# A four-layer graph network on one core: propagation slabs cut into 6-block pieces, and three small moves in TensorE's order

## The chip, the cores and the metric

The kernel runs on one core of one Trainium2 chip. The metric is the device time of one execution in microseconds; the time given for the kernel is the median of three runs. One execution was also taken with the hardware profiler, and every view quoted below comes from that one.

## The reference, cut to what matters

The input is x (3327 nodes of 256 features) and a dense adjacency matrix adj of 3327 x 3327, in float32. Each of four layers has the form x = x + layer(relu(layernorm(x)), adj):

```python
# layer 0:  adj @ (h @ W.T + b)
# layer 1:  relu(keep(tanh(adj * adj)) @ (tanh(h @ Wp + bp) @ Wg) + bg)   # keep: 700 largest of each row
# layer 2:  relu(A_norm @ (h @ W.T)),  A_norm = d^-1/2 (adj + I) d^-1/2
# layer 3:
R = S + jnp.eye(N); R = R / R.sum(-1, keepdims=True)      # S is adj
for n in range(2):
    A  = _top_p_attention(Xa, W1, W2, W3)   # softmax of q @ k.T, smallest set of 0.9, renormalized
    Xf = R @ Xf
    Xa = A @ Xa
    Z  = Z + Xf @ U1[n].T + Xa @ U2[n].T
# then layernorm(X + Z)
```

The change touches layer 3, where every step has a product with R ("propagation") and a product with the attention matrix A, and the order of a few steps in layers 1 and 2.

## The kernel before, in words

The 3327 nodes are padded to T = 26 row blocks of P = 128; H = 13 is half of that. The products of 26 x 26 blocks are done in halves of 13 blocks by a seven-product scheme: sums of quarter matrices are formed once and multiplied in products numbered 1 to 7, and the results are added up.

TensorE (PE) executes in an order that the program writes out by hand; the other engines' instructions are ordered by a scheduler at build time, from the program's priorities. All loads of R's blocks are issued on SyncE's (SP's) queue, in order: an issue that waits for a buffer holds up those behind it.

**Layers 0 to 2.** `products()` goes through H = 13 pairs of row blocks; a pair p is one `Product` in three cuts of the inner dimension (`CUTS`). Work of the pair before (turning its result with transposes, L418; projecting it) is hung into the current product's sequence as "hooks": a dictionary from step number to a function, called when PE's program reaches that step. For p = 1, part of whose product is already done during p = 0 (`early`), the hooks are carried into product p = 2, at the steps 10 and 34, and a counting hook at 22.

**Layer 3, first step.** Row block m of the attention is processed as follows. PE makes the logits (L1062), ScalarE (ACT) their exponentials (L1087), VectorE (DVE) finds the threshold and leaves the kept exponentials e_a (L1164). PE turns e_a block by block (L204), ACT copies the turned blocks to eT_a (L207), and PE multiplies them with the node features (L215). `rows.begin(m)` starts this with the first turned blocks, `rows.finish(m)` does the rest. After that the result's `turn`, `node` and `values` make the row's new keys and its share of Z.

Between the rows stand the phases of the propagation. `FirstPropagation(d)` for d = 0 to 5 is a "double", which handles two row blocks of each half at once; d = 6 is the "single". A double has four phases, groups of the seven products:

```python
OF_DOUBLE = (1, 2), (5, 4), (6, 3), (7,)
OF_LAST_DOUBLE = (1, 2), (5, 4), (6,), (3, 7)
OF_SINGLE = (1, 2, 5, 4), (6, 3, 7)
```

A phase of two products has 26 units, one of a single product 13; a unit of a double reads 128 KB of a slab and one of the single 64 KB. `propagate_first(n, at)` does phase n % 4 of double n // 4, with hooks `at` given on a scale of 26. The phases n = 0 to 3 run first, with little between them; n = 4 to 21 alternate with rows; n = 22 to 25 come with the last rows. In the alternating ones the hooks are, in this order, `a.turn`, the next row's preparation, `a.node`, `a.values` and `rows.begin(m + 1)`. After a phase, `keep()` adds its result up on DVE.

A slab of R comes from `adj_t` or, for products of sums of quarters, from `s_dram`, where layer 2 stored these sums. Where the slab has blocks of the diagonal, GpSimd (POOL) adds the identity to them (L1258). `load_slab` issues the DMA (L1253). The pool `slabs` has three buffers of 13 blocks, 832 KB each. A double cuts a product at `(0, 6, 12, 13)`: two slabs of 768 KB, and a last one for k = 12, shared by the phase's products, which takes a whole buffer too. Its units are sorted so that k = 12 comes last. The single and the pairs of step 2 use one slab of 832 KB for a product.

**Layer 3, second step.** The same attention per row; the propagation is done by `propagated_steps` (two row blocks) and by 12 `PropagatedPair` objects, each in two phases of 52 and 39 units that lie between rows.

The functions that the change touches:

Of the kernel before, what the change touches and what calls it, by code (L numbers as in the profile page):

```python
# [11 lines left out]
F32 = mybir.dt.float32  # L12
# [5 lines left out]
ALU = mybir.AluOpType  # L18
# [4 lines left out]
D = 256  # L23
# [7 lines left out]
H = T // 2  # L31
CUTS = ((0, 5), (5, 9), (9, 13))
TOPK = 700
TOP_P = 0.9
# [13 lines left out]
def kernel(  # L48
# [27 lines left out]
    keys = ctx.enter_context(tc.tile_pool(name="keys", bufs=1))  # L76
    slabs = ctx.enter_context(tc.tile_pool(name="slabs", bufs=3))
    ps_tr = ctx.enter_context(tc.tile_pool(name="ps_tr", bufs=2, space=PSUM))
# [78 lines left out]
    def slab_tile(name):  # L157
        return slabs.tile([P, H, P], F32, tag="slab", name=name)

# [134 lines left out]
    def layers_0_to_2(again):  # L294
# [343 lines left out]
        def products(layer, width, rhs, feed, finish, before, pair_after, following=None, counted=None, begin=None):  # L638
# [5 lines left out]
            for p in range(H):  # L644
# [4 lines left out]
                else:  # L649
# [8 lines left out]
                    if early and p == 1:  # L658
                        hooks, carried = {}, {10: todo[0], 34: todo[1]}
                    elif early and p == 2:  # L660
                        hooks.update(carried)
                    if counted and early and p == 1:
                        carried[22] = functools.partial(counted, p)
                    elif counted:
                        hooks[62] = functools.partial(counted, p)
# [331 lines left out]
    def layer_3_in(again, tag, big, ep, w3, sm3, h3, kT0, ksum0, left):  # L997
# [181 lines left out]
        def failed(step, st):  # L1179
# [27 lines left out]
            return levels  # L1207

        def propagated_steps(acc, step, m, xf):

            slab = {}
            order = [k for k in range(T) if k % H < H - 1] + [H - 1, T - 1]
            for n, k in enumerate(order):
                g, j = k // H, k % H
                if g not in slab:
                    s = slab[g] = slab_tile(f"slab3{tag}_{step}_{m}_{g}")
                    nc.sync.dma_start(s, adj_t[m, :, g * H : (g + 1) * H, :])
                    if m // H == g:
                        nc.gpsimd.tensor_tensor(s[:, m - g * H, :], s[:, m - g * H, :], ident, ALU.add)
                nc.tensor.matmul(acc[:, :D], slab[g][:, j, :], xf[:, k, :], start=(n == 0), stop=(n == T - 1))  # L1220
                yield n
# [3 lines left out]
        OF_DOUBLE = (1, 2), (5, 4), (6, 3), (7,)  # L1225
        OF_LAST_DOUBLE = (1, 2), (5, 4), (6,), (3, 7)
        OF_SINGLE = (1, 2, 5, 4), (6, 3, 7)
# [38 lines left out]

        class FirstPropagation:

            def __init__(self, d):
                self.d, self.p = d, 2 * d
                self.q = min(self.p + 2, H)
                self.many = self.q - self.p
                self.width = self.many * P
                self.phases = OF_SINGLE if self.many == 1 else OF_LAST_DOUBLE if d == DOUBLES - 1 else OF_DOUBLE
                self.cuts = (0, H) if self.many == 1 else (0, 6, 12, H)
                self.slabs, self.ys = {}, []
                self.name = f"0{tag}_{d}"

            def load(self, phase, n, c=0):
                a, b = self.cuts[c : c + 2]
                x = slab_tile(f"slab3{tag}_{self.name}_{n}_{c}")
                ns = self.phases[phase] if c == 2 else (n,)
                with tc.issue_after(slabs_behind[-1].ins) if slabs_behind else nullcontext():
                    for i, n in enumerate(ns):
                        part = x[:, i * self.many * (b - a) : (i + 1) * self.many * (b - a), :]
                        self.slabs[n, c] = part.rearrange("p (t k) m -> p t k m", t=self.many)
                        load_slab(self.slabs[n, c], n, self.p, self.q, a, b)

            def units(self, phase):
                units = [(n, k) for n in self.phases[phase] for k in range(H)]
                if self.many > 1:
                    units.sort(key=lambda u: u[1] == H - 1)
                return units

            def steps(self, phase):

                units = self.units(phase)
                place = {n: i for i, n in enumerate((2, 1, 4, 5) if self.many == 1 and not phase else  # L1300
                                                    {1: (2, 1), 5: (4, 5)}.get(units[0][0], self.phases[phase]))}
                self.acc = new_acc(f"f{self.name}_{phase}")
                self.at = {n: slice(c * self.width, (c + 1) * self.width) for n, c in place.items()}
                for at, (n, k) in enumerate(units):
                    c = sum(k >= b for b in self.cuts[1:-1])
                    if (n, c) not in self.slabs:
                        self.load(phase, n, c)
                    nc.tensor.matmul(  # L1308
                        self.acc[:, self.at[n]], right_half(h3, ts, n, k), self.slabs[n, c][:, :, k - self.cuts[c], :],
                        start=not at, stop=at == len(units) - 1, skip_group_check=True,  # L1310
                    )
                    yield at

            def keep(self, phase):
# [5 lines left out]
                with tc.high_priority():  # L1320
                    for k in range(0, len(ns), 2) if ns[0] == 1 or ns[0] == 5 else ():
                        y = w3.tile([P, 2, 2 * P], F32, tag="xf", name=f"y_{self.name}_{phase}_{k}", bufs=3)[:, :, :width]
                        self.ys.append(y)
                        nc.scalar.copy(
                            y, self.acc[:, k * width : (k + 2) * width].rearrange("p (n f) -> p n f", n=2)
                        )
                    for n in ns if ns[0] in (3, 6, 7) else ():
                        (y0, y1), b = self.ys, self.acc[:, self.at[n]].rearrange("p (n f) -> p n f", n=1)
                        if n == 6:
                            nc.vector.tensor_tensor(y0[:, 0:1, :], y0[:, 0:1, :], y0[:, 1:2, :], ALU.add)  # L1330
                            nc.vector.tensor_tensor(y0[:, 1:2, :], y0[:, 1:2, :], b, ALU.add)
                            nc.vector.tensor_tensor(y1, y1, both(y0[:, 1:2, :]), ALU.add)
                        elif n == 3:
                            nc.vector.tensor_tensor(y0[:, 1:2, :], y1[:, 1:2, :], b, ALU.add)
                        else:
                            nc.vector.tensor_tensor(y1, y1, both(b), ALU.add)
                if phase == len(self.phases) - 1:
                    for i, y in enumerate(self.ys):
                        for t in range(self.many):
                            props.append(PropagationOfFirstStep(self.p + t + i * H, y[:, :, t * P : (t + 1) * P]))  # L1340

        class PropagatedPair:


            def __init__(self, step, p, h, ts):
                self.step, self.p, self.h, self.ts = step, p, h, ts
                self.accs, self.slabs, self.name = {}, {}, f"{step}{tag}_{p}"
                self.last = p == H - 1

            def load(self, n):  # L1350
                x = self.slabs[n] = slab_tile(f"slab3{tag}_{self.step}_{self.p}_{n}")
                self.loaded = load_slab(
                    x.rearrange("p (t k) m -> p t k m", t=1), n, self.p, self.p + 1, 0, H
                )

            def steps(self, phase):

                units = [(n, k) for n in PHASES[phase] for k in range(H)]
                place = {**PLACE3, 3: (2, 0)} if self.last else PLACE3
                last = {place[n][0]: (n, k) for n, k in units}  # L1360
                for at, (n, k) in enumerate(units):
                    bank, c = place[n]
                    start = bank not in self.accs
                    if start:
                        self.accs[bank] = new_acc(f"f{self.name}_{bank}")
                    if n not in self.slabs:
                        self.load(n)
                    nc.tensor.matmul(
                        self.accs[bank][:, c * P : (c + 1) * P], self.slabs[n][:, k, :],
                        right_half(self.h, self.ts, n, k),  # L1370
# [316 lines left out]
        with tc.manual_schedule(engines=PE_ALONE):  # L1687
# [38 lines left out]
            firsts, fs = {}, []  # L1726

            def propagate_first(n, at):

# [68 lines left out]
            for m in range(T):  # L1798
# [11 lines left out]
                if interleaved:  # L1810
                    left_over = {}
                    steps, n = prepare(0, m + AHEAD, kT0), next(propagated)
                    at = (4, 14, 18, 22, 24) if n % 4 == 3 else (3, 10, 15, 18, 20)
                    what = a.turn, lambda: next(steps), a.node, a.values, lambda: rows.begin(m + 1)
# [229 lines left out]
```

## Time and profile before

| what | value |
|---|---|
| time, median of three runs | 2498.07 us (2497.99 to 2499.03) |
| profiled execution | 2498.93 us |
| its span | 2497.0 us |
| mean granted clock of PE | 0.998 |
| PE busy | 2471.1 us, 99% of the span |
| DVE busy | 2094.2 us, 84% |
| ACT busy | 1075.8 us, 43% |
| POOL busy | 287.6 us, 12% |
| DMA queue 1 | 367.53 MB, 45.8% of 16 engines |

The span is the profiler's time from the first to the last instruction; the execution's own time is 1.9 us longer. A busy share is an average over the whole kernel. Layers 0 to 2 take the span up to about 935 us, the first step of layer 3 up to about 1770, the second step the rest. "Idle before" in PE's timeline is time in which PE had no instruction in work, with what it waited for; these are the places to look at, since PE is busy for nearly all of the span.

### The profile page before, as it was taken

To read this page: it belongs to the slowest core of one execution; us is meant where nothing else is said; L and a number is where in the kernel's file an instruction comes from. 1 tells how busy PE (TensorE), PEld (TensorE's weight loads), DVE (VectorE), ACT (ScalarE), POOL (GpSimd) and SP (SyncE) were. 2 spreads that over 40 slices of the span, in tenths; PEclk is the share of its full clock that TensorE was granted. 3 is DMA by queue.
4 is the path that set the end of the run, shared out by engine and by line. 5 is a ranking of instruction groups with operands and counts; after the bars stand their busy time and mean duration, and the time that the engine had idled before them with its cause. 6 is when DMAs were issued, how large, how long until landed. Compare 5 with 4: busy or idle time off the path is not lost. (4 is left out here: it accounts for less than half of the span.)

```text
span 2497.0 us, 45220 instructions
## 1 busy us (share of the span) xinstructions
PE 2471.1 (99%) x16719; PEld 2187.2 (88%) x16719; DVE 2094.2 (84%) x5506; ACT 1075.8 (43%) x2109; POOL 287.6 (12%) x488
## 2 busy tenths in 40 slices
PE   9999999999999999999999999999999999999998
PEld 8999999999999997777777777777788888888887
DVE  7876788889888778888788797885899999999995
ACT  3101034443111115566566565663555655555551
POOL 2000010000000000000000000000022222332222
PEclk9999999999999999999999999999999999999999
DMA  6777765555688756323232323323533343344333
GB/s 202 228 231 239 222 199 179 181 175 181 227 304 294 258 192 214 103 80 104 84 96 83 120 67 115 103 64 121 179 115 114 125 142 114 117 140 143 125 118 115
DMA packets 196737, 387.90 MB, mean 155 GB/s; under 512 B 19997, under 2 KB 79898, under 8 KB 196506
## 3 DMA queue, kind: packets, MB, share of 16 engines
q1 hardware_dynamic: 175242, 367.53, 45.8%
q10 hardware_dynamic: 21264, 17.39, 2.1%
q8 instruction: 133, 2.18, 0.4%
q14 instruction: 98, 0.80, 0.1%
HBM read 315.24 MB, written 67.89 MB: 153 GB/s over the span
## 5 line engine op out<-in xcount | busy, mean ns | idle before, releaser
L207 ACT COPY eT_a<-pt_a 128x512 f32<-128x512 f32 (+1 forms) x364 | 196.3, 554 | 375.9 <-PE pt_a L204 373.5
L215 PE MATMUL a<-h3a,eT_a 128*128 128x256 f32 x1352 | 322.0, 381 | 3.2 <-ACT eT_a L207 3.2
L215 PE MATMUL a<-vs,eT_a 128*128 128x256 f32 x1352 | 320.2, 381 | 0.2 <-ACT eT_a L207 0.2
L215 PEld LDWEIGHTS a<-h3a,eT_a 128*128 128x128 f32 x1352 | 246.0, 189 | 48.3 <-issue 10.0
L1149 DVE MAX8 cand_a<-w 128x8 f32<-128x128 f32 x1352 | 284.6, 278 | 3.9
L215 PEld LDWEIGHTS a<-vs,eT_a 128*128 128x128 f32 x1352 | 244.9, 190 | 30.2 <-ACT eT_a L207 0.7
L602 PE MATMUL acc_a<-tsa,s_a 128*128 128x128 f32 (+1 forms) x2028 | 270.1, 275 | 0.0
L602 PE MATMUL acc_a<-tsa,a_a 128*128 128x128 f32 x2028 | 252.9, 276 | 0.0
L602 PEld LDWEIGHTS acc_a<-tsa,s_a 128*128 128x128 f32 x2028 | 249.0, 192 | 0.7
L602 PE MATMUL acc_a<-rhs,a_a 128*128 128x128 f32 (+1 forms) x2028 | 248.6, 276 | 0.0
L602 PEld LDWEIGHTS acc_a<-tsa,a_a 128*128 128x128 f32 x2028 | 241.1, 193 | 0.5
L602 PEld LDWEIGHTS acc_a<-rhs,a_a 128*128 128x128 f32 x2028 | 236.7, 192 | 0.6
L1145 DVE SCALAR_TENSOR_TENSOR w<-e_a,t_a 128x896 f32<-128x896 f32 x208 | 224.8, 1081 | 3.6
L1087 ACT ACTIVATE e_a<-pl_a 128x1024 f32<-128x1024 f32 x260 | 184.5, 728 | 43.5 <-PE pl_a L1062 43.4
L204 PE MATMUL pt_a<-ident,e_a 128*128 128x128 f32 x1352 | 198.4, 272 | 1.4 <-DVE e_a L1164 1.4
L1136 DVE SCALAR_TENSOR_TENSOR w<-e_a,t_a 128x3328 uint8<-128x3328 f32 x52 | 192.1, 3695 | 4.8 <-DVE t_a L1133 0.5
L1164 DVE SCALAR_TENSOR_TENSOR e_a<-e_a,all_least 128x3328 f32<-128x3328 f32 x52 | 192.1, 3695 | 1.8
L204 PEld LDWEIGHTS pt_a<-ident,e_a 128*128 128x128 f32 x1352 | 166.4, 141 | 31.1 <-issue 1.8
L422 ACT ACTIVATE xT_a<-pt_a 128x512 f32<-128x512 f32 x52 | 30.8, 593 | 334.5 <-PE pt_a L418 272.0
L754 ACT ACTIVATE a_a<-a_a 128x640 f32<-128x640 f32 (+1 forms) x156 | 101.6, 666 | 163.8 <-DVE a_a L752 149.8
L1308 PE MATMUL f0a<-slab3a_0a,tsa 128*128 128x256 f32 (+1 forms) x728 | 163.2, 368 | 3.8 <-POOL slab3a_0a L1258 2.5
L1120 ACT ACTIVATE junk_a<-e_a,t_a 128x3328 uint8<-128x3328 f32 x52 | 159.8, 3073 | 1.0 <-POOL parts_a L1082 0.6
(265 smaller groups left out, 4036.7 us busy)
## 6 DMA issues: line engine op xcount, KB each, us to landing
a_a<-in_adj_t_dram SPq DMA_DIRECT2D x312, 256.0 KB, 4.1
a_a<-in_adj_t_dram SPq DMA_DIRECT2D x156, 320.0 KB, 4.0
slab3a<-s_dram SPq DMA_DIRECT2D x48, 832.0 KB, 4.4
slab3a_0a<-s_dram SPq DMA_DIRECT2D x48, 768.0 KB, 4.7
slab3a<-in_adj_t_dram SPq DMA_DIRECT2D x40, 832.0 KB, 4.6
slab3a_0a<-in_adj_t_dram SPq DMA_DIRECT2D x36, 768.0 KB, 4.5
s_dram<-s_a SPq DMA_DIRECT2D x78, 256.0 KB, 5.0
s_dram<-s_a SPq DMA_DIRECT2D x39, 320.0 KB, 4.8
```

The costliest lines, as they stand in the source:

```text
L204: nc.tensor.transpose(pt[:, j, :], e[:, k * P : (k + 1) * P], ident)
L207: last_turned.append(nc.scalar.copy(eT[:, : len(blocks), :], pt[:, : len(blocks), :]))
L215: nc.tensor.matmul(acc[:, :width], ready[g][:, j, :], rhs[:, k, :], start=(k == 0), stop=(k == T - 1))
L602: nc.tensor.matmul(self.acc[:, g, at : at + wide], quads[n][:, k - CUTS[c][0], :], t, start=(k == 0 and n in (1, 4)), stop=(k == H - 1 and ...
L754: nc.scalar.activation(a, a, AF.Tanh)
L1087: last_exp.append(nc.scalar.activation(dst, src, AF.Exp, accum_out=parts[:, c : c + 1]))
L1120: nc.scalar.activation(junk_a, e, AF.Relu, scale=-1.0, bias=t, accum_out=short)
L1136: nc.vector.scalar_tensor_tensor(junk, e, t, e, ALU.is_lt, ALU.mult, accum_out=got)
L1145: nc.vector.scalar_tensor_tensor(w[:, : (b - a) * P], eg, t, eg, ALU.is_lt, ALU.mult, accum_out=below[:, g : g + 1])
L1149: nc.vector.max(cand[:, 8 * k : 8 * k + 8], w[:, (k - a) * P : (k - a + 1) * P])
L1164: nc.vector.scalar_tensor_tensor(e, e, least, e, ALU.is_ge, ALU.mult, accum_out=st["kept"][:, m : m + 1])
L1308: nc.tensor.matmul(self.acc[:, self.at[n]], right_half(h3, ts, n, k), self.slabs[n, c][:, :, k - self.cuts[c], :], start=not at, stop=at = ...
```

## The change

Five things are done:

1. The slabs' pool gets six buffers of 6 blocks (`PIECE = 6`) in place of three of 13. A phase's units are cut into pieces of 6 blocks, which is 3 units of a double or 6 of the single or a pair, whichever product they belong to. A piece that runs over the end of a product takes two DMAs. The units of a phase run in the order of the products; the sorting of k = 12 to the end is left only in the first phase of d = 0. A new class `Pieces` does this for `FirstPropagation` and `PropagatedPair`.
2. In the last double the phase `(6,)` becomes the second, before `(5, 4)`, so n = 21 has 13 units and n = 22 has 26. `keep()` splits its additions accordingly.
3. The hooks carried into product p = 2 in layers 1 and 2 move from steps 10, 34 and 22 to 18, 42 and 30.
4. In phases of one product (n % 4 = 3 before, and now n = 21 as well) `rows.begin(m + 1)` is called at 22 and `a.values` at 24, in place of the other way round.
5. Ahead of the single, four pieces are loaded in place of two slabs.

```diff
-    slabs = ctx.enter_context(tc.tile_pool(name="slabs", bufs=3))
+    slabs = ctx.enter_context(tc.tile_pool(name="slabs", bufs=6))
...
-        return slabs.tile([P, H, P], F32, tag="slab", name=name)
+        return slabs.tile([P, PIECE, P], F32, tag="slab", name=name)
...
-                        hooks, carried = {}, {10: todo[0], 34: todo[1]}
+                        hooks, carried = {}, {18: todo[0], 42: todo[1]}
...
-                        carried[22] = functools.partial(counted, p)
+                        carried[30] = functools.partial(counted, p)
...
-        OF_LAST_DOUBLE = (1, 2), (5, 4), (6,), (3, 7)
+        OF_LAST_DOUBLE = (1, 2), (6,), (5, 4), (3, 7)
...
+        class Pieces:
+            def load(self, phase, s):
+                units = self.units(phase)
+                per = PIECE // self.many
+                x, at = slab_tile(f"slab3{tag}_{self.name}_{phase}_{s}"), 0
+                for n, group in itertools.groupby(units[s * per : (s + 1) * per], lambda u: u[0]):
+                    for a, b in runs(k for _, k in group):
+                        size = self.many * (b - a)
+                        part = x[:, at : at + size, :].rearrange("p (t k) m -> p t k m", t=self.many)
+                        self.loaded = load_slab(part, n, self.p, self.p + self.many, a, b)
+                        for k in range(a, b):
+                            self.slabs[phase, n, k] = part[:, :, k - a, :]
+                        at += size
+
+            def block(self, phase, at):
+                n, k = self.units(phase)[at]
+                if (phase, n, k) not in self.slabs:
+                    self.load(phase, at // (PIECE // self.many))
+                return self.slabs[phase, n, k]
...
             def units(self, phase):
                 units = [(n, k) for n in self.phases[phase] for k in range(H)]
-                if self.many > 1:
+                if not self.d and not phase:
                     units.sort(key=lambda u: u[1] == H - 1)
                 return units
...
                     nc.tensor.matmul(
-                        self.acc[:, self.at[n]], right_half(h3, ts, n, k), self.slabs[n, c][:, :, k - self.cuts[c], :],
+                        self.acc[:, self.at[n]], right_half(h3, ts, n, k), self.block(phase, at),
...
+                        if n == 6 and y1 is not None:
                             nc.vector.tensor_tensor(y1, y1, both(y0[:, 1:2, :]), ALU.add)
...
+                    if phase and self.phases[phase - 1] == (6,):
+                        y0, y1 = self.ys
+                        nc.vector.tensor_tensor(y1, y1, both(y0[:, 1:2, :]), ALU.add)
...
-                    at = (4, 14, 18, 22, 24) if n % 4 == 3 else (3, 10, 15, 18, 20)
+                    at = (4, 14, 18, 24, 22) if len(products_of(n)) == 1 else (3, 10, 15, 18, 20)
...
-            for n in OF_SINGLE[0][:2]:
-                firsts[DOUBLES].load(0, n)
+            for s in range(4):
+                firsts[DOUBLES].load(0, s)
```

`propagated_steps` cuts its 26 units in the same way.

More of the change, by code (lines that the diff above doesn't have):

```diff
@@ L32 @@
 CUTS = ((0, 5), (5, 9), (9, 13))
+PIECE = 6
 TOPK = 700
@@ L1207, in failed, with runs @@
             return levels
+        def runs(ks):
+            out = []
+            for k in ks:
+                if out and out[-1][1] == k:
+                    out[-1][1] += 1
+                else:
+                    out.append([k, k + 1])
+            return out
         def propagated_steps(acc, step, m, xf):
-            slab = {}
             order = [k for k in range(T) if k % H < H - 1] + [H - 1, T - 1]
             for n, k in enumerate(order):
[L1214 to L1220, printed above, removed]
+                j = n % PIECE
+                if not j:
+                    piece = order[n : n + PIECE]
+                    s, at = slab_tile(f"slab3{tag}_{step}_{m}_{n}"), 0
+                    for a, b in runs(piece):
+                        nc.sync.dma_start(s[:, at : at + b - a, :], adj_t[m, :, a:b, :])
+                        at += b - a
+                    if m in piece:
+                        x = s[:, piece.index(m), :]
+                        nc.gpsimd.tensor_tensor(x, x, ident, ALU.add)
+                nc.tensor.matmul(acc[:, :D], s[:, j, :], xf[:, k, :], start=(n == 0), stop=(n == T - 1))
                 yield n
@@ L1265, in right_half @@
             return ts[:, {5: 0, 6: 1, 7: 2, 4: 3}[n], k, :]
-        class FirstPropagation:
+        class Pieces:
[16 more added lines that the diff above has]
+                return self.slabs[phase, n, k]
@@ L1271, in __init__ @@
+        class FirstPropagation(Pieces):
             def __init__(self, d):
                 self.d, self.p = d, 2 * d
-                self.q = min(self.p + 2, H)
-                self.many = self.q - self.p
+                self.many = min(2, H - self.p)
                 self.width = self.many * P
                 self.phases = OF_SINGLE if self.many == 1 else OF_LAST_DOUBLE if d == DOUBLES - 1 else OF_DOUBLE
-                self.cuts = (0, H) if self.many == 1 else (0, 6, 12, H)
                 self.slabs, self.ys = {}, []
@@ L1279, in __init__, with load @@
                 self.name = f"0{tag}_{d}"
[L1281 to L1284, printed above, removed]
+            def load(self, phase, s):
                 with tc.issue_after(slabs_behind[-1].ins) if slabs_behind else nullcontext():
[L1286 to L1289, printed above, removed]
+                    super().load(phase, s)
@@ L1304, in steps @@
                 for at, (n, k) in enumerate(units):
-                    c = sum(k >= b for b in self.cuts[1:-1])
-                    if (n, c) not in self.slabs:
-                        self.load(phase, n, c)
                     nc.tensor.matmul(
-                        self.acc[:, self.at[n]], right_half(h3, ts, n, k), self.slabs[n, c][:, :, k - self.cuts[c], :],
+                        self.acc[:, self.at[n]], right_half(h3, ts, n, k), self.block(phase, at),
                         start=not at, stop=at == len(units) - 1, skip_group_check=True,
@@ L1327, in keep @@
                     for n in ns if ns[0] in (3, 6, 7) else ():
-                        (y0, y1), b = self.ys, self.acc[:, self.at[n]].rearrange("p (n f) -> p n f", n=1)
+                        (y0, y1), b = (*self.ys, None)[:2], self.acc[:, self.at[n]].rearrange("p (n f) -> p n f", n=1)
                         if n == 6:
@@ L1334, in keep @@
                             nc.vector.tensor_tensor(y0[:, 1:2, :], y1[:, 1:2, :], b, ALU.add)
-                        else:
+                        elif n == 7:
                             nc.vector.tensor_tensor(y1, y1, both(b), ALU.add)
+                    if phase and self.phases[phase - 1] == (6,):
+                        y0, y1 = self.ys
+                        nc.vector.tensor_tensor(y1, y1, both(y0[:, 1:2, :]), ALU.add)
                 if phase == len(self.phases) - 1:
@@ L1340, in keep @@
                             props.append(PropagationOfFirstStep(self.p + t + i * H, y[:, :, t * P : (t + 1) * P]))
-        class PropagatedPair:
+        class PropagatedPair(Pieces):
             def __init__(self, step, p, h, ts):
@@ L1347, in __init__, with units @@
                 self.accs, self.slabs, self.name = {}, {}, f"{step}{tag}_{p}"
[L1348 to L1354, printed above, removed]
+                self.last, self.many = p == H - 1, 1
+            def units(self, phase):
+                return [(n, k) for n in PHASES[phase] for k in range(H)]
             def steps(self, phase):
-                units = [(n, k) for n in PHASES[phase] for k in range(H)]
+                units = self.units(phase)
                 place = {**PLACE3, 3: (2, 0)} if self.last else PLACE3
@@ L1365, in steps @@
                         self.accs[bank] = new_acc(f"f{self.name}_{bank}")
-                    if n not in self.slabs:
-                        self.load(n)
                     nc.tensor.matmul(
-                        self.accs[bank][:, c * P : (c + 1) * P], self.slabs[n][:, k, :],
+                        self.accs[bank][:, c * P : (c + 1) * P], self.block(phase, at)[:, 0, :],
                         right_half(self.h, self.ts, n, k),
@@ L1726, in layer_3_in, with products_of @@
             firsts, fs = {}, []
+            def products_of(n):
+                return (OF_LAST_DOUBLE if n // 4 == DOUBLES - 1 else OF_DOUBLE)[n % 4]
             def propagate_first(n, at):
```

## The prediction

> **What bounds the kernel now.** I read the page first, then the waits of TensorE (PE), then the stretches around the largest waits in PE's timeline and in windows with the granted clock. From the page:
>
> ```profile
> span 2497.0 us, 45220 instructions
> PE 2471.1 (99%) x16719; PEld 2187.2 (88%) x16719; DVE 2094.2 (84%) x5506; ACT 1075.8 (43%) x2109; POOL 287.6 (12%) x488
> ...
> slab3a_0a<-s_dram SPq DMA_DIRECT2D x48, 768.0 KB, 4.7
> ```
>
> PE is busy for all but 25.9 us of the span. So a change that leaves the matmuls as they are can win only what PE idles or runs slowly. About 10 us of these 25.9 are the end of the kernel after PE's last work (a chain of DVE, POOL and the output's DMA) and 1.5 the start, which the change does not touch. What is left, some 14 us, is listed by the view of the waits (engine, line waited for, total us, times, longest):
>
> ```profile
> PE a L215 <- ACT eT_a L207: 3.4, 11, 0.4
> PE f0a L1308 <- POOL slab3a_0a L1258: 2.5, 3, 1.7
> PE pt_a L418 <- DVE h3a L462: 1.9, 1, 1.9
> ...
> PE pt_a L204 <- DVE e_a L1164: 1.4, 1, 1.4
> PE f0a L1308 <- DMA slab3a_0a<-s_dram: 1.3, 1, 1.3
> PE f0a L1308 <- DMA slab3a_0a<-in_adj_t_dram: 1.1, 1, 1.1
> ```
>
> Where they lie, from PE's timeline (start, length, operation, the idle time before it in brackets):
>
> ```profile
> 694.26 0.66 PE L418 MATMUL pt_a<-ident,h3a 128*128 128x128 f32 x4 [1.90 <-DVE h3a L462]
> 695.88 3.35 PE L602 MATMUL acc_a<-tsa,a_a 128*128 128x128 f32 x16
> ...
> 949.01 0.70 PE L1308 MATMUL f0a<-slab3a_0a,tsa 128*128 128x256 f32 x2 [0.30 <-POOL slab3a_0a L1258]
> 950.21 1.56 PE L1308 MATMUL f0a<-slab3a_0a,tsa 128*128 128x256 f32 x6 [0.49 <-POOL slab3a_0a L1258]
> ...
> 966.00 1.99 PE L1308 MATMUL f0a<-slab3a_0a,tsa 128*128 128x256 f32 x8 [1.31 <-DMA slab3a_0a<-s_dram]
> ...
> 982.42 1.13 PE L1308 MATMUL f0a<-slab3a_0a,tsa 128*128 128x256 f32 x4 [1.74 <-POOL slab3a_0a L1258]
> ...
> 1739.70 2.50 PE L1308 MATMUL f0a<-slab3a_0a,h3a 128*128 128x128 f32 x20 [1.07 <-DMA slab3a_0a<-in_adj_t_dram]
> ```
>
> Each part of the change stands over one or more of these lines. The same view has the waits for eT_a (0.24 at 1138.5, for one) and for e_a (1.36 at 1702.5). The page's row of the granted clock, a 9 in every slice, is too coarse for what follows the first wait; windows around it (us, PE busy, PE weight loads, DVE, ACT, POOL, granted clock, DMA share, GB/s) show more:
>
> ```profile
> 688.00:692.00 4.00, 4.00 (x39) 4.00 (x38) 3.43 (x8) 0.48 (x1) 1.17 (x2) 1.00 1.02 335
> 692.00:695.40 3.40, 1.50 (x14) 1.31 (x13) 3.06 (x11) 0.44 (x1) 0.30 (x1) 1.00 0.98 367
> 695.40:698.80 3.40, 3.40 (x18) 3.40 (x17) 3.21 (x6) 0.15 (x1) 0.00 (x0) 0.50 0.95 301
> ```
>
> After the wait of 1.90 us PE runs 3.4 us at half clock: 18 matmuls where 3.4/4.00 of 39 would be 33.
>
> **The hooks of layers 1 and 2 (units 10, 34, 22 to 18, 42, 30).** The eight steps of a product between step 10 and step 18 are sixteen matmuls of L602 at about 0.11 us from start to start (20 take 2.40 in the same timeline, the last one's own 0.27 within it): about 1.6 us of PE work put ahead of the turn, the transposes L418. Their operand h3a is ready at 694.21; PE, which now comes at 692.36, comes at about 693.98 and still waits about 0.3. The product's next stretch (step 25 on) needs a combination s_a that DVE (L555) finishes at 696.81; without the long wait PE is there at about 696.06, a new wait of about 0.7. So 1.9 turns into 1.0. The half clock is the larger matter: a rule in the Trainium skill, "TensorE: Matmul & The Clock Gate" (table of Part 1), lets the clock fall after about 3.4 us of idling, and by it a wait of 1.9 us costs 1.9 and the hook is worth 0.9. The row above speaks against it: 1.90 us of waiting were followed by 3.4 us at 0.50, which costs another 1.7. No other wait here was followed by such a drop, the 1.74 one included; so I expect none behind 0.3 and 0.7, and count 0.9 + 1.7 = 2.6. In layer 1 the trace has no wait at the turn: nothing there, with matmuls to cover it on either side (the one wait of layer 1's product, 0.58 for s_a at 402, lies ahead of the hooks and stays).
>
> **The slabs in pieces.** Before, three buffers hold 768 KB (6 units of PE's 0.446 us, each 128 KB) or, for k = 12, only 512 KB in a whole buffer (256 KB in phase (7,)). The first slab of a next phase can be asked for only when the buffer three back is read out. Where phase follows phase with little between, that is about 6 units and a tail slab of 2 to 4 before the phase ends, and a slab takes 4.7 us median (up to 8.97 in this stage) plus POOL's addition of the identity. At 948.7, 949.7, 964.7 and 980.7 it is late: 0.30 + 0.49 + 1.31 + 1.74 = 3.83 us. After, a piece has 3 units and the piece in the freed buffer is needed 5 pieces, 15 units or 6.7 us of PE, later. I estimate its landing from two rows: 256 KB issued at 899.70 landed in 2.80 us and 768 KB in 4.7, so 384 KB in about 3.3, and with POOL's 0.46 under 4. Margin 2.7 us. The queue's bandwidth: PE asks 128 KB each 0.446 us, 294 GB/s, within a phase; the windows of 944 to 966 moved 239 to 274 GB/s with other loads (u1s, u2s) among them, so a phase of 26 units (11.6 us) falls behind by at most 10 to 20%, 1.2 to 2.3 us, inside the 6.7 of lead. All 3.83 us go; bounds 1.5 and 3.83.
>
> The rule that speaks against this part: "DMA: Bandwidth & Descriptors" (Bandwidth) asks for transfers of 1 MiB and more, and its anatomy's fit is 2.0 us + bytes/436 GB/s; halving 768 KB would drop the rate of a lone transfer from 206 to 134 GB/s, below PE's 294. If transfers ran one after the other, the four phases of d = 0 (91 units, 11.9 MB, 2.4 of it ahead) would need 9.5 MB / 134 GB/s = 71 us where PE takes 57 (934.9 to 991.5): an estimate of 14 us lost there, and a sum near 2508. The trace denies that they are serial: slabs were issued 0.86 us apart (947.88, 948.74) with landings of 7 and 9 us, and the stage moved up to 274 GB/s over 8 us. After, up to five pieces are in flight and the fixed part overlaps. I take nothing for it.
>
> Issue costs: a double's phase goes from 6 to 10 DMAs, (7,) from 3 to 5 or 6, a pair of step 1 from 7 to 21. At 0.32 to 0.38 us each on SP, the 12 pairs' 168 more take some 56 us of SP over 660 us; SP mostly waits there (534 us of its waits are for PE to release a slab). What is queued behind: the stores of z and u and the loads of x, which have tens of microseconds; and in the other direction a piece behind a store of z waits for DVE's z (27 us longest before). In the order of SP that the change gives, such stores stand between pieces 2 and 3 of a phase, and z is done before that phase begins since a row's transposes and values (about 20 us of PE) lie between. Nothing. POOL's additions are as many (a few doubled where a piece crosses products), and DVE's e_a, which a busier POOL could hold up, is ready 2.8 us or more before PE turns it, in all rows but 25 (0.15) and the last (0.23); PE has one wait of 0.24 in step 1.
>
> **Loads ahead of the single.** The 1.07 at 1738.6: pieces of 384 KB in six buffers are asked for from about 1729 on, land by about 1732.5 and are there. Gain 1.07.
>
> **The last double.** The short phase (6,) is now n = 21, the long one n = 22. Row 23, begun at the end of n = 21, is asked for 13 units (5.8 us) sooner; its e_a ends at 1647.73 and PE turns it at 1662.47, 14.7 ahead: no wait. DVE's one addition of 0.67 us comes a phase later. Row 25's wait of 1.36 is for DVE, whose e_a ends at 1703.72. PE's work until then is the same; DVE's chain begins about 0.45 earlier as the logits come earlier, and a 0.13 wait for the turn's copy goes. Gain 0.44; bounds -0.7 and 1.4.
>
> **The turned blocks ahead of the values.** The short phases n = 7, 11, 15, 19 have the 0.24 wait for ACT's first copy of eT_a (1138.5, 1284.7, 1431.0, 1577.5), since only a unit stands between the transposes and their use. Now the values' matmuls do too; n = 21 is handled likewise. Gain 4 x 0.24 = 0.95. The five waits of 0.39 after the rows alone (1077 ...) stay.
>
> **Sum.** 2.6 + 3.83 + 1.07 + 0.44 + 0.95 = 8.9 us against the profiled execution, 2498.93 (span 2497.0 and 1.9 around it): 2490.0. The three timed runs have their median at 2498.07; should the half clock not occur in those the sum is 7.2, and 2490.9. I predict 2490.5. A difference of 0.2%, 5.0 us, is about what a measurement of this kernel can tell from no change: faster is under 2493.1, slower over 2503.1.
>
> **The rivals.** First, **waits that take the place of those removed** (0.24). Row 0's e_a ends at 987.42 and PE needs it at 991.33, 3.91 of slack; 3.04 of the removed stalls lie between its logits and that point. 0.9 is left, and a POOL task ahead of it could eat this. Row 25 may get the DVE time back; step 1, where DVE is 95% busy, gives no more. If the d = 0 stage keeps half of its stalls and row 25 gains nothing, the sum is 8.9 - 1.9 - 0.44 - 1.0 (a hook's wait as long as before) = 5.6, and 3.9 from 2498.07 if the half clock's 1.7 is not in the timed runs: 2494. In favour: DVE is at 84% and every one of these chains ends in it. Against: 3.91 is more than 3.04.
>
> Second, **the small pieces become the bound** (0.12), the other side. Place: each interleaved phase of d = 1 to 5 and the 24 phases of step 1, which wait for no slab now (and d = 0 as above). It decides when a piece takes over 6.7 us from release to landing (issue in line on SP, 3.3, POOL's 0.46): by a store queued in between whose data is late, or the fixed 2 us not overlapping. One wait of 0.5 us in each of 18 + 24 phases is 21 us, minus the 8.9: 2510. Against it: the landing rows and DMA share of 0.3 in those slices.
>
> Third, **pieces bring nothing but the other edits do** (0.06): the stage of d = 0 is limited by the rate of DMA, not the depth. Then 8.9 - 3.83 = 5.1: 2493 to 2494.
>
> Main forecast 0.58. The range 2488 to 2500 takes in the first and third and the low end of nothing gained. Chances: faster 0.62 (main, and a little of the others), same 0.25, slower 0.13.
>
> **What would show it.** In the profile after: PE busy about 2469 to 2471 in a span of about 2488; no wait of L1308 for POOL or DMA at 945 to 985 and none near 1733; L418's wait for h3a below 0.5, a new L602 for s_a near 0.7, and granted clock 1.00 around 695; eT_a's waits seven, not eleven; L1164's wait about 1.0. I am wrong if L1308's or step 1's L1368's waits grow, or a wait for e_a at row 0 of over 1 us comes in, or if PE's busy time moves by more than 3 us with no clock drop to explain it.

## The result

The changed kernel takes 2493.16 us (median of ten runs, 2490.63 to 2499.26), the kernel before 2498.99 us in the runs beside it; the ratio is 0.9976, with a 95% interval of 0.9966 to 0.9985. It is faster by about 6 us. The prediction was 2490.5, with a range of 2488 to 2500.

From the page of the changed kernel's profile (one execution, 2492.22 us):

```profile
span 2490.1 us, 45726 instructions
PE 2467.9 (99%) x16719; PEld 2186.0 (88%) x16719; DVE 2100.5 (84%) x5506; ACT 1074.2 (43%) x2109; POOL 307.2 (12%) x488
```

The span is 6.9 us shorter, with PE's instructions unchanged in number. Two figures moved that the prediction had not forecast: DVE is busy 6.3 us longer and POOL 19.6 us longer, with as many instructions as before. That is a first hint that the two collide. (The line numbers are one to 25 higher than before: L1145 is now L1146, L1308 is L1333, L1368 is L1392.) PE's waits (line waited for, us, times, longest):

```profile
PE pt_a L205 <- DVE e_a L1165: 2.7, 2, 1.4
PE a L216 <- ACT eT_a L208: 2.4, 7, 0.4
...
PE acc_a L603 <- DVE s_a L556: 1.1, 2, 0.6
PE pk_mean_0a L1029 <- DVE ktotal_0a L1033: 0.5, 1, 0.5
```

No wait for a slab is left, none for h3a, and seven of the eleven for eT_a. The line at the top is the one to stop at: there are two waits for e_a where there was one. Read by the starts of PE's instructions at seven places, the difference between the two profiles is:

| stretch | before, us | after, us | difference |
|---|---|---|---|
| to the first slab matmul of layer 3 | 934.93 | 932.77 | -2.16 |
| from there to row 0 (the phases of d = 0) | 56.40 | 52.03 | -4.37 |
| row 0 to row 22 | 636.80 | 634.85 | -1.95 |
| row 22 to row 25 (the last double) | 75.74 | 75.23 | -0.51 |
| row 25 to the second step's row 0 (the single) | 69.51 | 68.17 | -1.34 |
| second step, row 0 to its last row | 687.93 | 689.44 | +1.51 |
| last row to the end | 35.70 | 37.60 | +1.90 |
| sum | 2497.01 | 2490.09 | -6.92 |

So 10.3 us were won before the second step, more than the 8.9 of the prediction, and 3.4 were given back in the second step, of which the prediction had nothing. The first row is not a gain to count on: over all the profiles taken here layer 3 begins between 932.60 and 934.93 us with the old hooks (four profiles) and between 931.94 and 934.51 with the new ones (nine). Where the last 1.9 went shows in the timeline of the end (start, length, engine, line; the idle time before it and what ended it in brackets):

```profile
2470.75 4.49 PE L1392 MATMUL f1a<-tsa,slab3a_1a 128*128 128x128 f32 x38
...
2470.95 0.61 SPq L1486 DMA_DIRECT2D u<-u_dram  x1
...
2471.61 0.42 SPq L1487 DMA_DIRECT2D x<-x_dram  x1
...
2474.67 0.72 POOL L1508 TENSOR_TENSOR x<-x,u1s 128x256 f32<-128x256 f32 x1 [15.33 <-DMA x<-x_dram]
...
2475.07 3.07 PE L1392 MATMUL f1a<-fsa,slab3a_1a 128*128 128x128 f32 x26
...
2478.85 0.72 POOL L1530 TENSOR_TENSOR z<-z,y 128x256 f32<-128x256 f32 x1
2479.61 0.48 DVE L1537 SCALAR_TENSOR_TENSOR z<-xf_1a,rinv,z 128x256 f32<-128x256 f32 x1 [2.46 <-POOL z L1530]
```

The same in the kernel before:

```profile
2458.15 7.00 SPq L1253 DMA_DIRECT2D slab3a<-s_dram  x3
...
2465.20 0.46 SPq L1462 DMA_DIRECT2D u<-u_dram  x1
...
2478.64 0.73 POOL L1474 TENSOR_TENSOR z<-z,y 128x256 f32<-128x256 f32 x1 [4.86 <-ACT y L1561]
...
2483.87 3.07 PE L1368 MATMUL f1a<-fsa,slab3a 128*128 128x128 f32 x26
...
2485.18 0.48 DVE L1513 SCALAR_TENSOR_TENSOR z<-xf_1a,rinv,z 128x256 f32<-128x256 f32 x1
```

Before, the loads of u, x and z that finish the last pair were issued from 2465.20 on, 21.7 us ahead of the end of PE's last product (2486.94), and POOL's last addition ended at 2479.4, 7.6 us ahead of it. In the changed kernel they go out from 2470.95 on, 7.2 us ahead of the product's end (2478.14), POOL's additions last until 2479.57, and DVE waits 2.46 us for them. The code says why: these loads are tied to `pair.loaded`, the last DMA that a pair issued. Before, that was the slab of the last product, issued at 2464.83, when the phase before had been read out and 13 us ahead of its own phase (2477.84). Now it is the last piece, number 6 of the phase, which waits on SP until PE has read piece 0 of the same phase. Piece 5 went out at 2456.11, piece 6 at 2470.58, and everything tied to it behind that.

The same lateness, in each of the earlier pairs, moves POOL's additions onto DVE's search for the threshold. DVE and POOL in the timeline, where DVE searches for the last row:

```profile
2423.16 3.68 DVE L1137 SCALAR_TENSOR_TENSOR w<-e_a,t_a 128x3328 uint8<-128x3328 f32 x1
...
2424.95 2.48 POOL L1560 TENSOR_TENSOR z<-z,u 128x256 f32<-128x256 f32 x1 [15.27 <-DMA u<-u_dram]
...
2426.89 0.56 DVE L1138 SCALAR_TENSOR_TENSOR u_a<-t_a,got_a 128x1 f32<-128x1 f32 x1
...
2427.80 0.46 DVE L1140 SCALAR_TENSOR_TENSOR t_a<-u_a,rate_a,t_a 128x1 f32<-128x1 f32 x1
...
2428.29 1.58 DVE L1146 SCALAR_TENSOR_TENSOR w<-e_a,t_a 128x896 f32<-128x896 f32 x1
2429.00 1.45 POOL L1561 TENSOR_TENSOR z<-z,y 128x256 f32<-128x256 f32 x1
```

The last three of DVE's instructions shown, in the same row of the kernel before:

```profile
2436.71 0.16 DVE L1137 SCALAR_TENSOR_TENSOR u_a<-t_a,got_a 128x1 f32<-128x1 f32 x1
...
2437.22 0.33 DVE L1139 SCALAR_TENSOR_TENSOR t_a<-u_a,rate_a,t_a 128x1 f32<-128x1 f32 x1
2437.59 1.15 DVE L1145 SCALAR_TENSOR_TENSOR w<-e_a,t_a 128x896 f32<-128x896 f32 x1
```

That is 0.96 us more for DVE. POOL's addition takes 2.48 where an undisturbed one takes 0.73. Eleven of DVE's 104 instructions of 896 columns were so lengthened to about 1.58, once a pair. Both engines are stretched while they overlap. From the start of that first 3.68 us instruction to the end of the row's e_a it takes 29.17 us instead of 28.09. The last row has no slack for this (before, PE took e_a up 0.23 us after its end, and where PE waits it is 0.15), and PE now waits:

```profile
2452.49 1.06 PE L205 MATMUL pt_a<-ident,e_a 128*128 128x128 f32 x8 [1.34 <-DVE e_a L1165]
```

### The profile page after: what moved, and what is told of

It reads as the page before. It is cut to its first block, busy times and chain, and to the rows that moved or that the text cites. A ratio compares the mean times of both kernels' runs of the same rounds, so it can differ in the third digit from the quotient of the medians.

```text
span 2490.1 us, 45726 instructions
## 1 busy us (share of the span) xinstructions
PE 2467.9 (99%) x16719; PEld 2186.0 (88%) x16719; DVE 2100.5 (84%) x5506; ACT 1074.2 (43%) x2109; POOL 307.2 (12%) x488
## 5 line engine op out<-in xcount | busy, mean ns | idle before, releaser
L1146 DVE SCALAR_TENSOR_TENSOR w<-e_a,t_a 128x896 f32<-128x896 f32 x208 | 229.6, 1104 | 3.6
L1333 PE MATMUL f0a<-slab3a_0a,tsa 128*128 128x256 f32 (+1 forms) x728 | 161.4, 367 | 0.0
```

The lines of the kernel that those rows point to most:

```text
L1146: nc.vector.scalar_tensor_tensor(w[:, : (b - a) * P], eg, t, eg, ALU.is_lt, ALU.mult, accum_out=below[:, g : g + 1])
L1333: nc.tensor.matmul(self.acc[:, self.at[n]], right_half(h3, ts, n, k), self.block(phase, at), start=not at, stop=at == len(units) - 1, skip ...
```

## The experiments

**The loads of z, u and x earlier.** First the explanation just given. One line of `Pieces.load` is changed: it no longer counts pieces 5 and 6 of the second phase as the last load. On SP the loads then stand directly behind piece 5; in each of the 12 pairs only piece 6 and these loads change places.

```diff
-                        self.loaded = load_slab(part, n, self.p, self.p + self.many, a, b)
+                        l = load_slab(part, n, self.p, self.p + self.many, a, b); self.loaded = self.loaded if phase and s > 4 else l
```

> The changed kernel, but the loads of z, u and x that finish a pair of the second step are queued on SP after piece 5 of the second phase instead of after its last piece 6; nothing else moves on PE. Theory (the loads stand behind a piece that waits for PE to release a buffer, 2470.58 instead of about 2456.5, so POOL's additions come late): the waits of DVE for POOL's z (2.46 us at the end) and of PE for e_a of the last row (1.31) shrink to under 0.5 each, L1146 of 896 columns goes back from 1.58 to 1.15 in the rows where POOL ran beside it, and the kernel is 3 to 4 us faster than the changed one, about 2489. Rival (the last row is bound by DVE and the end by PE's product whatever the loads do): the same time as the changed kernel within 0.5 us.

Measured: 2489.72 us (median of eight), 0.9958 of the kernel before (0.9943 to 0.9973), 3.4 us under the changed kernel's median; the span is 2485.6, 4.5 shorter. The two were timed apart and their intervals overlap a little (0.9966 to 0.9985 for the changed kernel). With each median set against that of the kernel before beside it, the gain is 8.3 us instead of 5.8. Of the two waits for e_a one is left, that of row 25:

```profile
PE pt_a L205 <- DVE e_a L1165: 1.3, 1, 1.3
```

The end of its timeline, where piece 6 now follows behind the loads:

```profile
2454.73 0.42 SPq L1486 DMA_DIRECT2D u<-u_dram  x1
...
2463.83 0.72 POOL L1530 TENSOR_TENSOR z<-z,y 128x256 f32<-128x256 f32 x1
...
2468.65 0.32 SPq L1267 DMA_DIRECT2D slab3a_1a<-s_dram  x1
...
2474.45 0.48 DVE L1537 SCALAR_TENSOR_TENSOR z<-xf_1a,rinv,z 128x256 f32<-128x256 f32 x1
```

The loads are out 21.5 us ahead of the end of PE's product (2476.21), as in the kernel before, DVE's wait for POOL is gone, and so is the wait for the last row's e_a; from the start of that row's search to the end of e_a it takes 28.10 us. DVE's rows of 896 columns are back at 1156 ns in the mean (1197 in the changed kernel, 1148 before). The second step, row 0 to last row, takes 688.03 us, as before (687.93).

**Only for the last pair.** The condition gets `and self.p == H - 1`.

> As the former, but only for the last pair. Theory: the end after PE's last product is 2.5 to 2.7 us shorter, the last row still waits 1.3 for e_a, since POOL's additions of the pairs before still run beside DVE: span about 2487.4. Rival (one cause behind both): the wait for e_a goes too.

Measured: span 2486.5, one run 2488.64 us. From the last row's start the end comes after 34.97 us instead of 37.60, and the wait for e_a stays:

```profile
PE pt_a L205 <- DVE e_a L1165: 2.6, 2, 1.4
```

So one cause, the late loads, has two effects that can be had apart: 2.6 at the end and about 1.3 in the last row. Its span was as low as it is partly because layer 3 began 0.8 us earlier than in the changed kernel (931.96), which no part of the edit touches.

**The hooks alone.** The kernel before with 18, 42 and 30 for 10, 34 and 22.

> The kernel before with the hooks of layers 1 and 2 moved to 18, 42 and 30 and nothing else. Theory: PE reaches layer 3 about 3 us earlier, the wait of 1.9 for h3a goes and with it the half clock after it, no other wait changes, and the end is 3 us earlier: 2495 to 2496. Rival (the layers' DVE takes the time back, or the half clock was not in the timed runs): 1 to 1.5 us, 2497.5.

Measured: 2497.4 us (ten runs), ratio 0.9992 (0.998 to 1.0003): no difference that can be told. Its waits:

```profile
PE acc_a L602 <- DVE s_a L555: 1.2, 2, 0.6
...
PE pt_a L418 <- DVE h3a L462: 0.9, 1, 0.9
PE pkq_a L271 <- DVE counts L737: 0.6, 1, 0.6
```

The wait for h3a is halved, not gone; the wait for s_a after it is there as forecast (0.60); and a third, for the counts whose hook went from 22 to 30, has come. Layer 3 begins at 934.51, 0.4 us earlier than in the kernel before, which had the half clock in addition.

**The old hooks in the best variant.** The counter-test, on the variant with early loads.

> The variant with early loads of z, u and x (2489.72 us), with the hooks back at 10, 34 and 22. Theory A (the half clock belongs to the wait of 1.9 for h3a): the wait of 1.5 to 1.9 and in most executions 3.4 us at half clock come back, the time is 3 us longer, 2492.5 to 2493. Theory B (the half clock in the profile of before was an occasional event, the hooks are worth only the waits): the wait comes back, the clock stays at 1.00, and the time is 1 to 1.5 us longer, about 2491.

Measured: 2489.03 us (five runs), beside 2489.72 with the new hooks; ratio 0.9962 (0.9949 to 0.9975). The wait is back, and the clock is not touched by it (windows: us, PE, PEld, DVE, ACT, POOL busy, granted clock, DMA share, GB/s):

```profile
692.00:695.40 3.40, 2.09 (x20) 1.90 (x18) 3.40 (x12) 0.60 (x1) 0.00 (x0) 1.00 0.93 343
695.40:698.80 3.40, 3.40 (x33) 3.39 (x32) 3.40 (x7) 0.00 (x0) 0.00 (x0) 1.00 0.99 318
```

Theory B holds in this profile, and even its 1 to 1.5 us are not seen in the times. In the four profiles that have the old hooks this wait was 1.90, 1.46, 1.23 and 1.31 us, and only the first, which is the profile that was predicted from, had the half clock.

**The pieces alone.** The kernel before with parts 1 and 5 of the change.

> The kernel before with the slabs in pieces and the four pieces ahead of the single, without the hooks, the last double's order and the turned blocks. Theory: the four waits of d = 0 and the one of the single go (start to start of the matmuls around them 4.5 and 1.3 us more than without a wait), so PE enters step 2 5.8 us earlier; then the end gives back 3 to 4 us by the late loads of z, u and x: in all 1.5 to 2.5 us faster than before, about 2496. Rival (pieces bring their whole gain): 5 to 6 us faster, 2493.

Measured: 2495.22 us (ten runs), ratio 0.999 (0.9978 to 1.0002): nearer to the theory's 1.5 to 2.5 us than to the rival's 5 to 6. The phases of d = 0 take 52.03 us and the single 68.17, as in the whole change, 5.7 us less than before; the waits for eT_a are eleven again, and the second step gives 4.2 back (1.8 up to its last row, 2.4 at the end). The waits of PE, and those of DVE near the end:

```profile
PE pt_a L205 <- DVE e_a L1165: 3.0, 2, 1.6
```

```profile
DVE z L1533 <- POOL z L1526: 2.5, 1, 2.5
```

**The turned blocks alone.** The kernel before with (4, 14, 18, 24, 22).

> The kernel before with only the order of the hooks in the phases n = 7, 11, 15, 19 changed (rows.begin at 22, a.values at 24). Theory (a wait costs what passes from start to start beyond the usual, 0.51 us instead of the 0.24 that is shown as idle): PE starts row 22 by 2.0 us earlier than in the kernel before, counted from its own start of layer 3; the four waits of 0.24 for eT_a are gone. Rival (the idle time is the cost): 0.95 us.

Measured: the four waits are gone, and row 0 to row 22 takes 634.85 us instead of 636.80, so 1.95 for 0.95 of idle time. The whole run was slower, 2500.91 us, for another reason: this execution waited 2.55 and 3.96 us for slabs at d = 0, and after each of these waits the clock fell. One of them in windows:

```profile
962.00:966.00 4.00, 1.45 (x8) 0.94 (x7) 3.89 (x5) 0.58 (x1) 0.00 (x0) 1.00 0.99 303
966.00:969.40 3.40, 3.40 (x9) 1.69 (x9) 3.29 (x11) 0.00 (x0) 0.00 (x0) 0.51 0.58 230
```

The stretch of d = 0 took 63.0 us there, 56.4 in the profile of before and 57.2 with the hooks alone. What the pieces remove is therefore not a fixed 4 us but a wait whose length changes from run to run.

**The last double in the old order,** in the variant with early loads, with `OF_LAST_DOUBLE` as before; `keep()` stays as changed, so it makes one addition of the last double twice.

> The variant with early loads of z, u and x, with the last double in the old order (1,2), (5,4), (6), (3,7). Theory: from PE's start of row 22 to that of row 25 it takes 0.5 to 0.6 us longer (75.7 instead of 75.14), a wait of 0.13 for ACT's xa comes back, and nothing else moves. Rival (the order also decides the single's first slab or row 23): a further difference of over 0.5 us between row 22 and row 26.

Measured: 75.76 us from row 22 to row 25 instead of 75.14, with the wait of 0.13 back, and 68.17 from there to the second step (68.24). As expected: this part is worth 0.5 to 0.6. The extra addition is not what makes the difference, since the pieces alone, with the old order and the old `keep()`, took 75.78.

**Depth.** The changed kernel with `bufs=4`, that is, pieces of the same size but 9 units of lead.

> The changed kernel with four buffers of 6 blocks instead of six. Theory (depth removes the slab waits: 15 units or 6.7 us of lead against landings of 4 us with POOL's addition): with four buffers the lead is 9 units or 4.0 us, slab waits return at d = 0, some 2 to 5 us in all, and a few of 0.1 to 0.5 elsewhere; the interleaved phases stay nearly free of them. Rival (the order across products and phases, not the depth, removed them): no wait of L1333 or L1392 for DMA or POOL over 0.3 us.

Measured: one run of 2520.58 us, span 2518.7, 28.6 longer. Waits of PE:

```profile
PE f0a L1333 <- POOL slab3a_0a L1272: 7.0, 4, 3.0
PE f1a L1392 <- POOL slab3a_1a L1272: 4.4, 7, 1.2
PE f0a L1333 <- DMA slab3a_0a<-s_dram: 3.5, 3, 1.5
```

At d = 0 it is as the theory has it: 56.43 us, 4.4 more than with six buffers. What it did not foresee is that the single and the second step wait too (the last double to the second step, rows 22 to 26, takes 153.2 us instead of 143.4, and the second step to its last row 697.9 instead of 689.4). A unit there (two matmuls of about 0.12 us) lasts 0.24 us, so 18 units of lead are about 4.3 us: no more than a landing of 3.8 to 5.0 us and, where it is needed, POOL's 0.46.

**Size at the same memory.** Early loads, with three pieces of 12 blocks and with nine of 4.

> The variant with early loads of z, u and x, with the same slab memory in three pieces of 12 blocks instead of six of 6 (two slabs instead of four pieces ahead of the single). Theory (what counts is how many units of the same memory are already asked for): a freed piece is needed 12 units or 5.4 us later and takes 4.7 us to land and 0.5 for POOL, so there are waits at d = 0 again, 1 to 3 us in all, most of them where another transfer is in flight, but less than before; span about 2488. Rival (pieces that run on across products are the whole gain, their size does not matter): no wait of L1333 for a slab, span within 0.5 us of 2485.6.

> The same with nine pieces of 4 blocks (2 units of a double, 256 KB), six pieces ahead of the single. Theory: lead of 16 units, 7.1 us, landings under 3.5 us: no slab waits; SP has half as many issues again, 0.35 us each, and still waits most of the time: the same time, 2489 to 2490. Rival (small transfers or SP's issuing become the bound): waits of L1333 or L1392 for DMA in many phases, over 2495.

Three of 12: one run of 2496.54 us, span 2494.6. The phases of d = 0 take 58.28 us, no less than before the change (56.40), with the waits at the same four places and a half clock after the last, of 1.81 (the third line is the single's wait):

```profile
PE f0a L1333 <- POOL slab3a_0a L1272: 2.6, 3, 1.8
...
PE f0a L1333 <- DMA slab3a_0a<-s_dram: 1.4, 1, 1.4
...
PE f0a L1333 <- DMA slab3a_0a<-in_adj_t_dram: 0.9, 1, 0.9
```

So in this one run to let pieces run across products, by itself, brings nothing at d = 0, and more waits came than the 1 to 3 us that were expected. Nine of 4: 2489.23 us (five runs), ratio 0.9965 (0.9951 to 0.998), no wait for a slab, the phases of d = 0 at 52.28. Transfers of 256 KB with 0.35 us of issuing each are no bound here; below 6 blocks there is nothing more to win either.

**One step further.** Early loads, and in the five iterations without a propagation phase `rows.begin(m + 1)` at 4 instead of 5.

> The variant with early loads of z, u and x, with rows.begin(m + 1) at 4 instead of 5 in the five iterations without a propagation phase, so that six matmuls instead of two stand between the first turned blocks and their use. Theory: the five waits of 0.39 for eT_a go, 0.55 each from start to start, 2.7 us in all, about 2487; PE's wait for e_a of row 25 stays at 1.3, since its chain starts from PE's logits. Rival (DVE's chains hold row 25 and the last row): the wait of row 25 grows by as much, 2489.5.

Measured: 2493.79 us (twelve runs), 4 us slower than without it. Its waits:

```profile
PE pt_a L205 <- ACT e_a L1088: 4.3, 5, 0.9
PE pt_a L205 <- DVE e_a L1165: 2.6, 1, 2.6
```

Five of the seven waits for eT_a went, but the transposes now stand directly behind the logits of another row and wait 0.86 us for ACT's exponentials, five times; and row 25 waits 1.3 longer. Neither theory foresaw the first. So the variant with early loads stays ahead of this one and of both kernels; the old hooks and nine pieces on top of it are as fast as it is, within what the runs can tell.

## Why the prediction came out as it did

The direction and the place of each gain were right. The forecast of 2490.5 was 2.7 us too low: it had 7.6 us of gain from 2498.07, and 5.8 were measured from 2498.99. A term that it set to nothing cost 2.5 to 4.5 us, and two errors of size on other terms cancel.

- **Issue costs and what is queued behind, set to nothing: this is the step that failed.** The prediction looked for stores ahead of pieces, and said of "the loads of x" that they "have tens of microseconds". It did not ask what these loads are tied to. They cost 1.34 us of waiting in the last row and about 2.6 at the end: issued behind piece 5, 4.5 us of span and 3.4 of median come back (2.5 when each is set against the runs beside it). The second rival named this place, SP's line, but as late slabs; no slab was late.
- **The slabs of d = 0, 3.83: right, 4.37 measured.** The margin argument (15 units against a landing) held: 384 KB landed in 3.8 to 4.0 us, against an estimate of 3.3. The rule that speaks against small transfers was set aside rightly: the kernel with pieces of 256 KB is as fast. (The fit quoted with it is for transfers that GpSimd issues; these are issued on SP.) The third rival, a stage bound by DMA's rate, is ruled out by the same rows: no wait for a slab was left.
- **The single, 1.07: right, 1.34. The turned blocks, 0.95: 1.95, half the size.** The reason is the same: the idle time of the profile begins where the modelled end of the last matmul is, which overlaps the next one (a matmul of 0.38 us starts 0.22 after the one before). The four waits of 0.24 for eT_a cost 0.49 each, and the slab waits at d = 0, counted from start to start beyond the usual 0.22, sum to 4.5, not 3.83.
- **The hooks, 2.6: the mis-sized term in the other direction.** The 1.7 for the half clock is in one of the four profiles with the old hooks, and the new waits (0.9 for h3a, 0.6 for s_a, up to 0.6 for the counts, which the prediction had not listed) left 0.4 us to the start of layer 3 in either pair of profiles (the kernel before and its hooks alone; the best variant with old and new hooks), less than that start varies among profiles with the same hooks, and nothing that can be told in the times.
- **The last double, 0.44: 0.5 to 0.6.** Row 25's wait stayed (1.37 us; 1.39 before, for which the prediction has 1.36); the gain is in front of it.
- **Row 0's e_a: the lead of 0.9 us that the first rival was left with is what the profile shows,** e_a ready at 983.90 and PE at 984.80. That rival did not come in.

The over-estimate of the hooks (about 2) and the under-estimates of the waits (about 2) cancel, which is luck; what is left is the second step. Of the signs named ahead, those of the slabs, of h3a, of s_a (0.6), of the clock at 695 and of eT_a came; that of e_a (about 1.0) did not, with 2.7 in two waits. Two slips of the working change nothing: the windows of 944 to 966 moved 231 to 274 GB/s, not 239, and the fit quoted gives an estimate of 135 GB/s for 384 KB, not 134.

## What to carry to other kernels

When a load is cut into pieces, look at everything that was tied to "the last load": the last piece is issued when its buffer comes free, much later than a whole slab was, and whatever follows in the same queue is late with it. The same memory, cut into more and smaller buffers, buys lead, up to the point where a landing is covered; beyond that, and in bigger pieces, nothing. Price a wait of a pipelined engine from start to start, and ask of a rare event in a single profile, a clock drop above all, whether the timed runs have it.

## What the runs showed of the hardware

Apart from the kernel's first 50 us and its end, the half clock lasted 3.41 us in the records (6.8 once) and came after waits of PE of 1.81, 1.90, 2.55, 2.79 and 3.96 us, and during one of 3.03; one of 2.62 had none, and of 28 between 1.0 and 1.74 us none had it, save one of 1.45 that stood directly ahead of the 3.03. So a good deal less than the 3.4 us of the Trainium skill ("TensorE: Matmul & The Clock Gate", Part 1) can be enough; what decides between 2.55 and 2.62 stays open. Nor is the half clock confined to single profiles: of the 50 timed executions of the kernel before that stand beside the experiments, seven have a mean granted clock of 0.997 (2500.2 to 2507.9 us), lower than the 10 us behind PE's last product can make it at half clock (0.998); the 18 of the variants with early loads and the new hooks, the old hooks or nine pieces all have 0.999. Where it fell in those seven no trace shows.

While POOL adds 128 x 256 tiles, DVE's two-input instruction of 896 columns took 1.58 instead of 1.15 us and POOL's addition 1.45 to 2.48 instead of 0.73. The Trainium skill, "SBUF — State Buffer" (Terms), describes a pair of ports for which the two engines take turns, each for a whole instruction; the rows agree, since POOL's 2.48 ends (2427.43) after DVE's instruction that ran beside it from 2423.16 to 2426.84, and DVE's next one is stretched to 0.56.
